# Layer b's scores in four row strips of the array, with one ring of five PSUM banks and a rearranged written order

## The chip, the cores and the metric

One core of a Trainium2 chip runs the whole program. The engines are TensorE (PE in the profile; its weight loads are PEld), VectorE (DVE), ScalarE (ACT), GpSimd (POOL) and SyncE (SP), which issues most of the DMA transfers. The metric is device microseconds of one execution. The kernel before took 4026.98 us, the median of three runs (4023.04 to 4030.02).

## The reference, cut to what matters

The input is four sequences of 2048 rows of 512 numbers. Four residual layers follow one another: layer a (linear attention), a feed-forward layer with int8 levels, layer b, and the same feed-forward layer again. The change touches layer b:

```python
g = sigmoid((x @ g_w.T + g_b).reshape(b, t, h, r))
decay = sigmoid(base_decay_logits)[None, :, :, None]
def step(M, inp):
    q_t, k_t, v_t, g_t = inp
    M = M * decay + einsum('bhr,bhd->bhrd', g_t * k_t * scale, v_t)
    y = einsum('bhr,bhrd->bhd', q_t, M)
    return (M, y)
```

There are 16 heads (h), each with a state of 16 x 32 (r x d), which decays at every row. q and k have 16 numbers per head and row. The outputs y of all rows go through a 512 x 512 product, are added to the row, and the sum is normalized.

## The kernel before, in words

All heavy arithmetic is in f32. Layer a with its feed-forward layer takes the first 2.4 ms of the span; layer b with its own runs from about 2450 us to the end. Layer b works on 32 blocks of 256 rows (NB = 4 sequences, 8 blocks each). A block has two halves of 128 rows (index i) and two groups of 8 heads (index g), so four **chunks**, numbered c = 2i + g. A sequence start clears the state (L1442).

A chunk does not step row by row. Within 128 rows, q and k are scaled by powers of the decay, and the chunk's work is:

- **scores** (L1318 to L1336): for each head, k times q over its 16 numbers gives a 128 x 128 matrix. A group's 8 heads lie on the 128 partitions, 16 apiece. Before the change, the scores are two matmuls (L1326), one for each half of the partitions: the stationary operand is k (64 rows by 128 columns, four heads in one), the moving one is q four times over (64 x 512), each copy zeroed by a mask for all heads but one (`q1`, L1294, with `head4`). Each fills one PSUM bank of `s`, which has two banks. Then L1333 starts the outputs `pyT` with the state's part, also in 64-row halves.
- **mask**: VectorE multiplies both banks by the causal triangle into `ab` (L1339), the last lines of `scores`.
- **update** (L1353, L1357): the state's growth, `pub`, added to `pairs`.
- **outputs** (L1366): scores times v, in 32-column strips, added to `pyT`; ScalarE copies it to `yT` (L1373), and GpSimd makes the next state (L1374).

The dense products of a block are features q and k for two groups (`pr`, L1230, 3.46 us of TensorE each), gates (`pg`) and the small maps `pl` (L1263), values (`pvb`, copied to `vb` by ScalarE, L1212), the output projection `py` (L1386) and the feed-forward product `pf` (L681). Each takes a PSUM bank from a ring with the tag `mm`, of three banks: a product's first matmul waits until the bank's holder three turns earlier has been read.

`prepare` (L1276 to L1303) makes the scaled operands of a group: k1 (L1282) and qs (L1288) on VectorE, q1 on ScalarE (L1294), ke and q0 on GpSimd (L1298). `turn_keys` then splits ke into 16-bit planes on VectorE (L710) and has SP's queue transpose them; `turned_keys` joins them on ScalarE (L717, kt). `turn_row` joins a transposed input row (xnTb, L717 too) and adds two biases on GpSimd (L1205, L1206).

The order on TensorE, VectorE, ScalarE and GpSimd is written by hand: within `tc.manual_schedule` an engine executes its instructions in the order in which `blocks_of(n)` issues them. In one call, `B` is the block whose chunks run, `after` the next (its features, gates, values and `prepare`), `later` the one after that (its rows are normalized and transposed), `before` the last (its output, normalization and feed-forward layer). Between two chunks' scores stand:

- chunk 0: features q 0, outputs of chunk 0, `levels(before, 0)`, features k 0, project(before, 1)
- chunk 1: weigh_output, gates and keys 0, outputs, `pf` of row 0, features q 1
- chunk 2: prepare 0, weigh_ffn, turn_row 0, values 0, turn_keys 0, outputs, `levels(before, 1)`, features k 1, project(B, 0)
- chunk 3: weigh_output, gates and keys 1, outputs, `pf` of row 1, store, prepare 1, turn_row 1, norm_output, turn_keys 1, values 1

Of the kernel before, what the change touches and what calls it, by code (L numbers as in the profile page):

```python
# [19 lines left out]
P = 128  # L20
# [12 lines left out]
HB, DB, R = 16, 32, 16  # L33
G = 2
HG = HB // G
# [6 lines left out]
QB = 128  # L42
NQ = P // QB
# [3 lines left out]
def hybrid_block_kernel(ctx: ExitStack, tc: tile.TileContext, t: dict, out: bass.AP):  # L47
# [4 lines left out]
    nc = tc.nc  # L52
    x_in = t["x"]
    NB, SEQ, _ = x_in.shape
# [581 lines left out]
    def run(steps):  # L636
        for f in steps:
            f()
# [432 lines left out]
    def layer_b_mild():  # L1071
        with ExitStack() as es:
# [4 lines left out]
            w = es.enter_context(tc.tile_pool(name="mb_w", bufs=1, reuse_waits="tile"))  # L1077
            pool = es.enter_context(tc.tile_pool(name="mb", bufs=2, reuse_waits="tile"))
            psum = es.enter_context(tc.tile_pool(name="mb_ps", bufs=1, space=PSUM, reuse_waits="tile"))

            bank = banks(psum, mm=3, s=2, y=2, u=1)
            at = [(b, blk) for b in range(NB) for blk in range(SEQ // TB)]

            def load_x(n):
# [20 lines left out]
                low[name] = soon.tile([P, 2, G, 2, 64], F32, name=f"low_{name}")  # L1105
                nc.sync.dma_start(low[name], t[f"m_{name}low"])
            small = {}
            for name in ("b_gb", "b_decay", "head4", "diag", "causal"):
                small[name] = w.tile(list(t[name].shape), F32, name=f"m_{name}")
                nc.sync.dma_start(small[name], t[name])  # L1110
            nc.sync.dma_start(wv, t["b_vT"].rearrange("(c p) n -> p c n", p=P))
# [164 lines left out]
            def prepare(B, g):  # L1276


                q, k = B.qk[g]
                A = Block()  # L1280
                A.k1 = pool.tile([P, NTB, NQ, P], F32, name=f"k1{g}", bufs=1)
                nc.vector.tensor_tensor(  # L1282
                    A.k1,
                    k.rearrange("p (i s) -> p i s", s=P).unsqueeze(2).to_broadcast([P, NTB, NQ, P]),
                    tk[:, g, :, :].unsqueeze(1).to_broadcast([P, NTB, NQ, P]), ALU.mult,
                )
                qs = pool.tile([P, NTB * NQ, QB], F32, name="qs", bufs=1)
                nc.vector.tensor_tensor(  # L1288
                    qs, q.rearrange("p (j s) -> p j s", s=QB),
                    tq[:, g, :].unsqueeze(1).to_broadcast([P, NTB * NQ, QB]), ALU.mult,  # L1290
                )
                A.q1 = pool.tile([P, NTB * NQ, 4, QB], F32, name=f"q1{g}", bufs=1)
                for h in range(4):
                    nc.scalar.activation(A.q1[:, :, h, :], qs, AF.Copy, scale=small["head4"][:, h : h + 1])  # L1294
                A.ke = pool.tile([P, NTB, P], F32, name="ke", bufs=1)
                A.q0 = pool.tile([P, NTB, P], F32, name=f"q0{g}", bufs=1)
                for dst, src, tab in ((A.ke, k, down), (A.q0, q, up)):
                    nc.gpsimd.tensor_tensor(  # L1298
                        dst, src.rearrange("p (i s) -> p i s", s=P),
                        tab[:, g, 1 : P + 1].unsqueeze(1).to_broadcast([P, NTB, P]), ALU.mult,  # L1300
                    )
# [11 lines left out]
            def chunk(B, i, g):  # L1313
# [4 lines left out]
                def scores():  # L1318


                    A = B.prep[g]
                    ps = [bank([P, NQ, 4, QB], F32, name="ps", tag="s") for _ in range(2)]
                    for j in range(NQ):
                        for half in range(2):
                            r = slice(half * 64, (half + 1) * 64)
                            nc.tensor.matmul(  # L1326
                                ps[half][:, j, :, :], A.k1[r, i, j, :], A.q1[r, NQ * i + j, :, :],
                                start=True, stop=True,
                            )
                    C.py = [bank([P, P], F32, name="pyT", tag="y") for _ in range(2)]  # L1330
                    for half in range(2):
                        r = slice(half * 64, (half + 1) * 64)
                        nc.tensor.matmul(  # L1333
                            C.py[half], st[r, half * P : (half + 1) * P], A.q0[r, i, :],
                            start=True, stop=False, skip_group_check=True,
                        )  # L1336
                    C.a = pool.tile([P, 2, 4, P], F32, name="ab")
                    for half in range(2):
                        nc.vector.tensor_tensor(  # L1339
                            C.a[:, half, :, :].rearrange("p h (j s) -> p h j s", s=QB),  # L1340
                            ps[half].rearrange("p j h s -> p h j s"),
                            small["causal"].rearrange("p (j s) -> p j s", s=QB).unsqueeze(1)
                            .to_broadcast([P, 4, NQ, QB]),
                            ALU.mult,
                        )

                def update():
# [13 lines left out]
                def outputs():  # L1361

                    for half in range(2):
                        for h in range(4):
                            lo = g * HG * DB + (4 * half + h) * DB
                            nc.tensor.matmul(  # L1366
                                C.py[half][h * DB : (h + 1) * DB, :], B.v[:, i, lo : lo + DB],
                                C.a[:, half, h, :], start=False, stop=True, skip_group_check=True,
                            )
                    if g == 0:  # L1370
                        B.yT[i] = pool.tile([P, KC, P], F32, name="yT", bufs=3)
                    for half in range(2):
                        nc.scalar.copy(B.yT[i][:, 2 * g + half, :], C.py[half])  # L1373
                    nc.gpsimd.tensor_tensor(  # L1374
                        st.rearrange("p (q c) -> p q c", c=2 * DB),
                        pairs[:, g, :].unsqueeze(1).to_broadcast([P, HG // 2, 2 * DB]),
                        small["diag"].rearrange("p (q c) -> p q c", c=2 * DB), ALU.mult,
                    )

                return scores, lambda: run([update, outputs])  # L1380

            def project(B, i):

# [1 line left out]
                for c in range(KC):  # L1385
                    nc.tensor.matmul(py, B.yT[i][:, c, :], wo[:, c, :], start=(c == 0), stop=(c == KC - 1))  # L1386

            def weigh_output(B, i):
                h = B.h[i] = pool.tile([P, D], F32, name="h")
                nc.vector.tensor_tensor(h, B.py.pop(i), B.xr[:, i, :], ALU.add)  # L1390
                B.stats[i] = stats(pool, h.unsqueeze(1), 1)

            def norm_output(B, i):
                h, x = B.h.pop(i), B.x[:, i, :]
# [43 lines left out]
            def blocks_of(n):  # L1438
# [3 lines left out]
                    nc.gpsimd.memset(state, 0.0)  # L1442
                    nc.gpsimd.memset(pairs, 0.0)
                nothing = lambda: None
                chunks = [chunk(B, c // G, c % G) if B else (nothing, nothing) for c in range(2 * G)]


                if B:
                    turned_keys(B, 0)
                chunks[0][0]()  # L1450
                if before:
                    weigh_ffn(before, 0)
                if after:
                    run(features(after, "q", 0))
                chunks[0][1]()
                if later:
                    weigh_row(later, 0)
                if before:
# [8 lines left out]
                    turned_keys(B, 1)  # L1467
                chunks[1][0]()
                if before:
                    weigh_output(before, 1)  # L1470
                if after:
                    run(gates(after, 0) + keys(after, 0))
                chunks[1][1]()
                if before:
                    run(before.levels[0])
                if later:
# [3 lines left out]
                if later:  # L1480
                    weigh_row(later, 1)
                if after:
                    run(features(after, "q", 1))


                chunks[2][0]()
                if after:
                    prepare(after, 0)
                if before:
                    weigh_ffn(before, 1)  # L1490
                if later:
                    turn_row(later, 0)
                if after:
                    run(values(after, 0))
                    turn_keys(after, 0)
                chunks[2][1]()
                if later:
                    norm_row(later, 1)
                if before:
# [7 lines left out]

                chunks[3][0]()
                if B:
                    weigh_output(B, 0)  # L1510
                if after:
                    run(gates(after, 1) + keys(after, 1))
                chunks[3][1]()
                if before:
                    run(before.levels[1])
                    store(before)
                if after:
                    prepare(after, 1)
                if later:
                    turn_row(later, 1)  # L1520
                if B:
                    norm_output(B, 0)
                if after:
# [17 lines left out]
def _constants(seq):  # L1541
# [10 lines left out]
        "head": (p[:, None] // R == np.arange(HG)[None, :]).astype(f),  # L1552
        "sub": (p[:, None] // SUB == np.arange(NS)[None, :]).astype(f),
        "diag": (p[:, None] // R == np.arange(HG * DB)[None, :] // DB).astype(f),
        "head4": (p[:, None] // R % 4 == np.arange(4)[None, :]).astype(f),
# [89 lines left out]
```

## Time and profile before

| what | value |
|---|---|
| median of three runs | 4026.98 us |
| the profiled execution | 4025.24 us |
| its span in the trace | 4023.4 us |
| granted TensorE clock, mean | 0.987 |
| one full block of layer b, scores to scores | 46.53 us |
| TensorE, VectorE, ScalarE, GpSimd busy in 2560 to 3950 us (1390 us) | 1356.2, 999.7, 325.9, 721.3 us |
| score matmuls L1326 | 512 records, 4 a chunk, 144.5 us busy |
| masks L1339 | 256, 684 ns each |
| q1 copies L1294 | 256, 497 ns each |

A line of the timeline gives start, length, engine, source line, operation, the tiles written and read, shapes and count; a bracket gives the engine's idle time just before, and what ended it. An f32 matmul leaves two records, one for each pass. A record's length contains the pipeline's tail, so that the distance of starts tells the time that a matmul takes from TensorE. Some tile names lose their numbers: `q<-qs,m_head` is q1, `k<-k,tk` is k1, `q<-q,up` is q0.

### The profile page before, as it was taken

The page shows a single profiled execution, that of the slowest core. Times are in us where ns is not written, and L with a number is a line of the kernel's source. Part 1 is how long each engine was busy: PE and PEld are TensorE (multiplying, and loading weights), DVE is VectorE, ACT ScalarE, POOL GpSimd, SP SyncE. Part 2 cuts the span into 40 slices and gives each one's busy share as a digit, 9 for nine tenths or more (in the row PEclk, how much of TensorE's full clock was granted, in tenths as well). Part 3 has the DMA queues.
Part 4 walks back from the last instruction along what each step waited for, and adds up shares of the span by engine and source line. Part 5 has one row for each costly group of instructions (what it writes and reads, how often), then busy time and mean ns, then how long its engine had stood idle before and what let it go on. Part 6 is the DMA issues. An engine that isn't in the chain of part 4 may idle for free.

```text
span 4023.4 us, 53593 instructions
## 1 busy us (share of the span) xinstructions
PE 3896.8 (97%) x20821; PEld 2133.2 (53%) x20821; DVE 2401.1 (60%) x4556; ACT 877.8 (22%) x1548; POOL 1516.3 (38%) x2527
## 2 busy tenths in 40 slices
PE   8999999999999999999999996999999999999996
PEld 4554554555554554555554544666556656665563
DVE  4455555555555555555555455677677767776775
ACT  2222222122122222222222211222222222222221
POOL 3233223323323322322332222455455545554553
PEclk9999999999999999999999997999999999999998
DMA  4122222212212212212212123122112111222111
GB/s 137 30 43 56 62 41 56 65 39 58 65 36 61 62 36 61 62 39 62 58 39 63 44 49 123 36 51 54 50 48 59 49 48 48 52 54 48 51 36 28
DMA packets 432040, 217.25 MB, mean 54 GB/s; under 512 B 363808, under 2 KB 376992, under 8 KB 431776
## 3 DMA queue, kind: packets, MB, share of 16 engines
q1 hardware_dynamic: 430656, 212.16, 21.7%
q8 instruction: 166, 2.72, 0.3%
q10 hardware_dynamic: 1120, 1.57, 0.1%
q14 instruction: 98, 0.80, 0.1%
HBM read 91.49 MB, written 34.08 MB: 31 GB/s over the span
## 4 chain that ended last, share of the span: by engine, by line
PE 90%; DVE 3%; ACT 2%; POOL 2%; DMA 2%; issue 1%; SPq 0%; ACTq 0%; POOLq 0%; DVEq 0%
PE pr L1230 12%; PE pk L648 11%; PE pv L648 11%; PE pq L648 11%; PE po L648 11%; PE py L1386 5%; PE pss L888 3%; PE pn L974 3%; PE pvb L648 3%; PE pg L648 3%; PE pl L1263 3%; PE pf L681 3%; PE pn L968 3%; PE ps L1326 3%; PE pu L904 2%
## 5 line engine op out<-in xcount | busy, mean ns | idle before, releaser
L648 PE MATMUL pq<-xnTa,a_Wq 128*128 128x512 f32 x1024 | 492.2, 608 | 0.0
L648 PE MATMUL pk<-xnTa,a_Wk 128*128 128x512 f32 x1024 | 491.0, 604 | 0.0
L126 POOL TENSOR_SCALAR rs<-mv 128x1 f32<-128x1 f32 x320 | 81.9, 256 | 1055.3 <-DVE mv L125 1052.2
L648 PE MATMUL pv<-a_Wv,xnTa 128*128 128x512 f32 x1024 | 476.3, 603 | 2.9 <-ACT xnTa L141 2.9
L648 PE MATMUL po<-a_Wo_sb,oT 128*128 128x512 f32 x1024 | 467.7, 601 | 6.4 <-DVE oT L950 6.4
L914 POOL TENSOR_TENSOR within<-state,u 64x64 f32<-64x64 f32 x256 | 155.8, 609 | 523.7 <-ACT u L909 514.1
L648 PEld LDWEIGHTS po<-a_Wo_sb,oT 128*128 128x128 f32 x1024 | 189.5, 190 | 235.3 <-issue 220.0
L648 PEld LDWEIGHTS pv<-a_Wv,xnTa 128*128 128x128 f32 x1024 | 188.7, 191 | 234.4 <-issue 224.2
L648 PEld LDWEIGHTS pq<-xnTa,a_Wq 128*128 128x128 f32 x1024 | 181.4, 189 | 193.1 <-issue 182.8
L648 PEld LDWEIGHTS pk<-xnTa,a_Wk 128*128 128x128 f32 x1024 | 184.5, 189 | 180.9 <-issue 158.8
L909 ACT COPY u<-pu 128x256 f32<-128x256 f32 x128 | 47.7, 373 | 1027.2 <-PE pu L904 1016.2
L1230 PE MATMUL pr<-xnTb,m_qT_sb 128*128 128x256 f32 x1024 | 240.6, 389 | 18.7 <-ACT xnTb L717 18.7
L1339 DVE TENSOR_TENSOR ab<-ps,m_causal 128x512 f32<-128x512 f32 x256 | 164.5, 684 | 131.6 <-PE ps L1326 131.6
L1230 PE MATMUL pr<-xnTb,m_kT_sb 128*128 128x256 f32 x1024 | 237.9, 385 | 0.0
L894 DVE TENSOR_TENSOR sm<-pss,causal 128x512 f32<-128x512 f32 x256 | 164.2, 683 | 119.4 <-PE pss L888 119.4
L648 PE MATMUL pvb<-b_vT_sb,xnTb 128*128 128x512 f32 x512 | 234.6, 601 | 0.0
L1386 PE MATMUL py<-b_oT_sb,yT 128*128 128x512 f32 x512 | 232.2, 596 | 0.0
L717 ACT COPY kr<-turned 128x1024 uint16<-128x1024 uint16 x120 | 139.3, 1161 | 425.6 <-DMA turned<-planes 425.6
L1230 PEld LDWEIGHTS pr<-xnTb,m_qT_sb 128*128 128x128 f32 x1024 | 196.1, 194 | 54.4 <-ACT xnTb L717 23.7
L683 DVE SCALAR_TENSOR_TENSOR f_y<-pf,f_sc,rscale 128x512 f32<-128x512 f32 x128 | 96.0, 750 | 198.3 <-PE pf L681 198.1
L1230 PEld LDWEIGHTS pr<-xnTb,m_kT_sb 128*128 128x128 f32 x1024 | 189.4, 190 | 35.6 <-issue 12.3
L127 POOL TENSOR_TENSOR rs<-rs,neg_half 128x1 f32<-128x1 f32 x320 | 193.1, 604 | 26.3
(158 smaller groups left out, 6304.0 us busy)
## 6 DMA issues: line engine op xcount, KB each, us to landing
wide<-rec SPq DMA_DIRECT2D x124, 256.0 KB, 3.7
mmid<-xa SPq DMA_DIRECT2D x16, 1024.0 KB, 4.3
out<-xb SPq DMA_DIRECT2D x32, 512.0 KB, 2.8
xa<-in_x SPq DMA_DIRECT2D x15, 1024.0 KB, 6.7
xb<-mmid SPq DMA_DIRECT2D x30, 512.0 KB, 3.8
turned<-planes SPq DMA_TRANSPOSE x304, 3.1
m_cos<-in_cos SPq DMA_DIRECT2D x30, 128.0 KB, 2.5
m_sin<-in_sin SPq DMA_DIRECT2D x30, 128.0 KB, 2.3
```

Source lines behind the costliest of these rows:

```text
L127: nc.gpsimd.tensor_tensor(rs, rs, neg_half[:, :n], ALU.pow)
L648: nc.tensor.matmul(held[0], lhs(), rhs(), start=(n == 0), stop=(n == len(pairs) - 1))
L681: nc.tensor.matmul(pf, qT[:, c, :], rq[:, c, :], start=(c == 0), stop=(c == KC - 1))
L717: nc.scalar.copy(dst.bitcast(U16).rearrange("p n (t two) -> p n t two", two=2), turned.rearrange("p (two n) t -> p n t two", two=2),)
L888: nc.tensor.matmul(ps[h][:, i, :], k[r, chunks[i]], q[r, chunks[i]], start=True, stop=True)
L894: nc.vector.tensor_tensor(s, ps[h], causal.unsqueeze(1).to_broadcast([P, NTA, P]), ALU.mult)
L914: nc.gpsimd.tensor_tensor(A.before[i + 1][r, r], A.before[i][r, r], u[r, i, :], ALU.add)
L968: nc.tensor.matmul(pn[:, i, :], A.before[i], q[:, chunks[i]], start=(i == 0), stop=False, skip_group_check=True,)
L974: nc.tensor.matmul(pn[r, i, :], v()[:, i, vh[h]], A.sm[h][:, i, :], start=False, stop=True, skip_group_check=True,)
L1230: nc.tensor.matmul(pr[:, half, :], wp[name][:, c, lo : lo + P], B.xnT[:, c, :], start=(c == 0), stop=(c == KC - 1),)
L1339: nc.vector.tensor_tensor(C.a[:, half, :, :].rearrange("p h (j s) -> p h j s", s=QB), ps[half].rearrange("p j h s -> p h j s"), small["cau ...
L1386: nc.tensor.matmul(py, B.yT[i][:, c, :], wo[:, c, :], start=(c == 0), stop=(c == KC - 1))
```

## The change

Each chunk's scores become four matmuls, one for each quarter (32 rows, two heads) of the partitions: k 32 x 128 stationary, q twice over moving (32 x 256, with `head2` in place of `head4`), each into a bank of its own. The banks for scores join those of the dense products in one ring of five, taken in the order in which the tiles are asked for. The mask becomes a step of its own, with four operations of 256 in place of two of 512; add_output, the sum of `py` and the row, is parted from weigh_output and goes ahead of the mask in chunks 1 and 3. values 0 and features q 1 change places. prepare 0 goes from chunk 2 to chunk 3 (behind the mask), turn_keys 0 from chunk 2 to the end of chunk 3, and turn_row 1 ahead of prepare 1.

```diff
-            bank = banks(psum, mm=3, s=2, y=2, u=1)
+            ring = banks(psum, mm=5, y=2, u=1)
+            def bank(shape, dtype, name, tag):
+                return ring(shape, dtype, name, "mm" if tag == "s" else tag)
...
-                for h in range(4):
-                    nc.scalar.activation(A.q1[:, :, h, :], qs, AF.Copy, scale=small["head4"][:, h : h + 1])
+                for h in range(2):
+                    nc.scalar.activation(A.q1[:, :, h, :], qs, AF.Copy, scale=small["head2"][:, h : h + 1])
...
-                    ps = [bank([P, NQ, 4, QB], F32, name="ps", tag="s") for _ in range(2)]
-                    for j in range(NQ):
-                        for half in range(2):
-                            r = slice(half * 64, (half + 1) * 64)
-                            nc.tensor.matmul(
-                                ps[half][:, j, :, :], A.k1[r, i, j, :], A.q1[r, NQ * i + j, :, :],
-                                start=True, stop=True,
-                            )
+                    C.ps = [bank([P, 2, P], F32, name="ps", tag="s") for _ in range(HG // 2)]
+                    for n in range(HG // 2):
+                        r = slice(n * 2 * R, (n + 1) * 2 * R)
+                        nc.tensor.matmul(C.ps[n], A.k1[r, i, :], A.q1[r, i, :, :], start=True, stop=True)
...
+                def mask():
+                    C.a = pool.tile([P, HG, P], F32, name="ab")
+                    for n in range(HG // 2):
+                        nc.vector.tensor_tensor(
+                            C.a[:, 2 * n : 2 * n + 2, :], C.ps[n],
+                            small["causal"].unsqueeze(1).to_broadcast([P, 2, P]), ALU.mult,
+                        )
...
                 chunks[1][0]()
                 if before:
+                    add_output(before, 1)
+                chunks[1][1]()
+                if before:
                     weigh_output(before, 1)
...
                 if after:
-                    run(features(after, "q", 1))
+                    run(values(after, 0))
                 chunks[2][0]()
-                if after:
-                    prepare(after, 0)
+                chunks[2][1]()
                 if before:
                     weigh_ffn(before, 1)
                 if later:
                     turn_row(later, 0)
                 if after:
-                    run(values(after, 0))
-                    turn_keys(after, 0)
-                chunks[2][1]()
+                    run(features(after, "q", 1))
+                chunks[2][2]()
...
                 chunks[3][0]()
                 if B:
+                    add_output(B, 0)
+                chunks[3][1]()
+                if B:
                     weigh_output(B, 0)
                 if after:
+                    prepare(after, 0)
                     run(gates(after, 1) + keys(after, 1))
-                chunks[3][1]()
+                chunks[3][2]()
                 if before:
                     run(before.levels[1])
                     store(before)
-                if after:
-                    prepare(after, 1)
                 if later:
                     turn_row(later, 1)
+                if after:
+                    turn_keys(after, 0)
+                    prepare(after, 1)
                 if B:
                     norm_output(B, 0)
```

More of the change, by code (lines that the diff above doesn't have):

```diff
@@ L1107, in layer_b_mild @@
             small = {}
-            for name in ("b_gb", "b_decay", "head4", "diag", "causal"):
+            for name in ("b_gb", "b_decay", "head2", "diag", "causal"):
                 small[name] = w.tile(list(t[name].shape), F32, name=f"m_{name}")
@@ L1280, in prepare @@
                 A = Block()
[L1281 to L1285, printed above, removed]
-                )
[L1287 to L1292, printed above, removed]
-                for h in range(4):
-                    nc.scalar.activation(A.q1[:, :, h, :], qs, AF.Copy, scale=small["head4"][:, h : h + 1])
+                A.k1 = pool.tile([P, NTB, P], F32, name=f"k1{g}", bufs=1)
+                qs = pool.tile([P, NTB, P], F32, name="qs", bufs=1)
+                for dst, src, tab in ((A.k1, k, tk[:, g, 0, :]), (qs, q, tq[:, g, :])):
+                    nc.vector.tensor_tensor(
+                        dst, src.rearrange("p (i s) -> p i s", s=P),
+                        tab.unsqueeze(1).to_broadcast([P, NTB, P]), ALU.mult,
+                    )
+                A.q1 = pool.tile([P, NTB, 2, P], F32, name=f"q1{g}", bufs=1)
+                for h in range(2):
+                    nc.scalar.activation(A.q1[:, :, h, :], qs, AF.Copy, scale=small["head2"][:, h : h + 1])
                 A.ke = pool.tile([P, NTB, P], F32, name="ke", bufs=1)
@@ L1321, in scores @@
                     A = B.prep[g]
-                    ps = [bank([P, NQ, 4, QB], F32, name="ps", tag="s") for _ in range(2)]
-                    for j in range(NQ):
-                        for half in range(2):
-                            r = slice(half * 64, (half + 1) * 64)
-                            nc.tensor.matmul(
-                                ps[half][:, j, :, :], A.k1[r, i, j, :], A.q1[r, NQ * i + j, :, :],
-                                start=True, stop=True,
-                            )
+                    C.ps = [bank([P, 2, P], F32, name="ps", tag="s") for _ in range(HG // 2)]
+                    for n in range(HG // 2):
+                        r = slice(n * 2 * R, (n + 1) * 2 * R)
+                        nc.tensor.matmul(C.ps[n], A.k1[r, i, :], A.q1[r, i, :, :], start=True, stop=True)
                     C.py = [bank([P, P], F32, name="pyT", tag="y") for _ in range(2)]
@@ L1336, in scores @@
                         )
-                    C.a = pool.tile([P, 2, 4, P], F32, name="ab")
-                    for half in range(2):
+                def mask():
+                    C.a = pool.tile([P, HG, P], F32, name="ab")
+                    for n in range(HG // 2):
                         nc.vector.tensor_tensor(
[L1340 to L1344, printed above, removed]
+                            C.a[:, 2 * n : 2 * n + 2, :], C.ps[n],
+                            small["causal"].unsqueeze(1).to_broadcast([P, 2, P]), ALU.mult,
                         )
@@ L1367, in outputs @@
                                 C.py[half][h * DB : (h + 1) * DB, :], B.v[:, i, lo : lo + DB],
-                                C.a[:, half, h, :], start=False, stop=True, skip_group_check=True,
+                                C.a[:, 4 * half + h, :], start=False, stop=True, skip_group_check=True,
                             )
@@ L1378, in outputs @@
                     )
-                return scores, lambda: run([update, outputs])
+                return scores, mask, lambda: run([update, outputs])
             def project(B, i):
@@ L1386, in project, with add_output, weigh_output @@
                     nc.tensor.matmul(py, B.yT[i][:, c, :], wo[:, c, :], start=(c == 0), stop=(c == KC - 1))
-            def weigh_output(B, i):
+            def add_output(B, i):
                 h = B.h[i] = pool.tile([P, D], F32, name="h")
                 nc.vector.tensor_tensor(h, B.py.pop(i), B.xr[:, i, :], ALU.add)
-                B.stats[i] = stats(pool, h.unsqueeze(1), 1)
+            def weigh_output(B, i):
+                B.stats[i] = stats(pool, B.h[i].unsqueeze(1), 1)
             def norm_output(B, i):
@@ L1444, in blocks_of @@
                 nothing = lambda: None
-                chunks = [chunk(B, c // G, c % G) if B else (nothing, nothing) for c in range(2 * G)]
+                chunks = [chunk(B, c // G, c % G) if B else (nothing, nothing, nothing) for c in range(2 * G)]
                 if B:
@@ L1450, in blocks_of @@
                 chunks[0][0]()
+                chunks[0][1]()
                 if before:
@@ L1454, in blocks_of @@
                     run(features(after, "q", 0))
-                chunks[0][1]()
+                chunks[0][2]()
                 if later:
@@ L1472, in blocks_of @@
                     run(gates(after, 0) + keys(after, 0))
-                chunks[1][1]()
+                chunks[1][2]()
                 if before:
@@ L1554, in _constants @@
         "diag": (p[:, None] // R == np.arange(HG * DB)[None, :] // DB).astype(f),
-        "head4": (p[:, None] // R % 4 == np.arange(4)[None, :]).astype(f),
+        "head2": (p[:, None] // R % 2 == np.arange(2)[None, :]).astype(f),
         "sin2": np.ascontiguousarray(
```

## The prediction

> **What bounds the kernel now.** I read the page's busy shares first, then the chain that ended last, then TensorE's waits from 2100 us on (where layer b lies), and last the timeline of single chunks.
>
> ```profile
> PE 3896.8 (97%) x20821; PEld 2133.2 (53%) x20821; DVE 2401.1 (60%) x4556; ACT 877.8 (22%) x1548; POOL 1516.3 (38%) x2527
> PE 90%; DVE 3%; ACT 2%; POOL 2%; DMA 2%; issue 1%; SPq 0%; ACTq 0%; POOLq 0%; DVEq 0%
> ```
>
> TensorE is busy 97% of the span and makes 90% of the chain. Inside layer b (the stretch 2560 to 3950 us) it is 1356.2 of 1390 us, with VectorE at 999.7 (72%) and GpSimd at 721.3 (52%). So a nanosecond off TensorE counts, unless another engine then comes late. What it waits for there:
>
> ```profile
> PE pr L1230 <- ACT xnTb L717: 18.7, 26, 0.7
> PE pyT L1333 <- POOL state_b L1442: 15.1, 3, 5.0
> PE pyT L1366 <- DVE ab L1339: 4.1, 6, 2.5
> ```
>
> Columns: us in all, times, longest. The first is one wait in nearly every block. The second is at the three later sequence starts. The third is the scores' mask, and the timeline puts it in the last block; in full blocks no mask is late.
>
> Layer b goes in blocks of four chunks. From the starts of L1326, chunk to chunk: 10.19, 12.68, 10.17, 13.49 us, 46.53 a block, the same to 0.01 us all along. The stretches of 12.68 and 13.49 hold the same amount of TensorE work (scores, three dense products of 3.45 us, outputs), so the first wait costs 0.81 us a block.
>
> **Part 1: the score matmuls.** The timeline of one chunk (start, length, engine, line):
>
> ```profile
> 3007.44 1.13 PE L1326 MATMUL ps<-q,k 64*128 64x512 f32 x4
> 3008.41 0.39 PE L1333 MATMUL pyT<-q,state_b 64*128 64x128 f32 x4
> 3008.72 1.99 PE L648 MATMUL pg<-xnTb,b_gT_sb 128*128 128x256 f32 x8
> 3010.65 0.65 PE L1263 MATMUL pl<-xc_q,low_q 128*64 128x256 f32 x4
> 3011.13 0.60 PE L1263 MATMUL pl<-xs_q,low_q 128*64 128x256 f32 x4
> ```
>
> Read starts, not lengths (lengths contain the pipeline's tail). An f32 matmul is two passes. The later L1263 groups, each two matmuls side by side on half arrays, follow every 0.43 us (3011.13, 3011.56, 3011.99): one 256-wide pass streams in 0.215 us, a 512-wide one in 0.43. py before them (eight 512-wide passes) takes 3.52 us from 3003.92 to 3007.44, 0.08 more than 8 x 0.43: about 0.09 us goes wherever the shape of the used array changes. The first group after such a change is also longer: 0.48 instead of 0.43, its second weights (64 columns) being loaded in the open; with 128 columns I take 0.11. The scores fit: 3007.44 to 3008.41 is 0.97 = 2 x 0.43 + 0.11, two 64-row matmuls abreast. L1333 follows in the same shape without the 0.09; it and its change to pg take 0.31.
>
> After: four matmuls of 32 rows, 256 wide, into four banks. If all four run abreast: 0.43 + 0.11, and 0.02 for staggered starts, is 0.56. Then a shape change that was not there, 32 to 64 rows: 0.09, and L1333's second load in the open, 0.05. So 0.56 + 0.14 + 0.31 = 1.01 instead of 1.28: **0.27 us saved a chunk**. The trace has pairs of row strips abreast (L1326, L1333) and quads of column strips (L1353, L1366), no quads of row strips. Bounds: with no price for the added change 0.41 saved; as two pairs one after the other 0.43 more streaming, so 0.16 lost; one by one 1.02 lost. I take 0.27, since pairs of both kinds and column quads run abreast.
>
> The skill has a rule against the part: the Trainium skill, "TensorEngine Tiling (Array Packing)", Key Properties, says that a change of tiling mode drains TensorE; "TensorE: Matmul & The Clock Gate", Single matmul latency, has a drain of about 175 ns. By that the added change would cost 0.175 in place of the rows' 0.09, an estimate of 0.19 saved a chunk instead of 0.27.
>
> **Part 2: masks and copies.** Two masks of 512 (0.684 us each) become four of 256; the nearest row is L1271, 256 wide and also from PSUM, at 0.42. Two started 0.61 apart, four should start 0.34 apart: 1.44 instead of 1.29 us on VectorE, +0.15 a chunk. Between mask and outputs TensorE has 3.5 us of dense work, so that hides; uncovered it would be 0.15 a chunk. ScalarE's copies of q per prepare go from four to two (0.43 each apart).
>
> The same tiling page's PSUM Bottleneck section warns that emptying PSUM can become the bound once matmuls are packed. By the page the masks would have to be late; in this trace VectorE waits for the scores (131.6 us over L1339), not TensorE for masks.
>
> **Part 3: the block's seam, where order and banks decide.** Around the start of a block:
>
> ```profile
> 3014.09 3.60 PE L648 MATMUL pvb<-b_vT_sb,xnTb 128*128 128x512 f32 x8
> 3014.29 0.75 DVE L683 SCALAR_TENSOR_TENSOR f_y<-pf,f_sc,rscale 128x512 f32<-128x512 f32 x1 [0.57 <-PE pf L681]
> 3014.96 0.41 DVE L1282 TENSOR_TENSOR k<-k,tk 128x256 f32<-128x256 f32 x1
> 3015.12 1.38 POOL L684 TENSOR_TENSOR xb<-xb,f_y 128x512 f32<-128x512 f32 x1 [0.60 <-DVE f_y L683]
> 3015.29 1.49 DVE L1288 TENSOR_TENSOR qs<-q,tq 128x256 f32<-128x256 f32 x1
> 3016.45 0.82 POOL L1298 TENSOR_TENSOR ke<-k,down 128x256 f32<-128x256 f32 x1
> 3016.87 1.71 ACT L1294 ACTIVATE q<-qs,m_head 128x256 f32<-128x256 f32 x4 [3.26 <-DVE qs L1288]
> 3017.61 1.13 PE L1326 MATMUL ps<-q,k 64*128 64x512 f32 x4
> 3018.48 1.15 ACT L717 COPY xnTb<-turned 128x1024 uint16<-128x1024 uint16 x1
> 3019.54 0.57 ACT L1212 COPY vb<-pvb 128x512 f32<-128x512 f32 x1
> ```
>
> L1288 takes 0.41 where GpSimd is quiet (start 3044.72) and 1.49 here: it ends 0.28 after GpSimd's add (3016.50). VectorE operations on two SBUF tiles, and copies, take turns with GpSimd's adds, each holding the other off. ScalarE waits for qs, copies four times, then turns xnTb; TensorE's next product starts at 3019.68, 5.59 after pvb's start.
>
> After, the turn of xnTb stands ahead of prepare: its wait goes. But the five-bank ring gives the product after the seam pvb's own bank (one turn later: pvb, four score tiles, then that product), so it now waits for vb's copy, and that stands on ScalarE behind the two q copies of prepare. From pvb's start: f_y ends at 0.95. VectorE now first turns ke (the moved step): it starts at 0.87 as L1282 did, 0.41 long, to 1.28. GpSimd's add ends 1.13 later, 2.41 (as 3015.37 to 3016.50). k1 to 2.70. GpSimd's next is now the ln_b add, alone 1.27, after a hold 1.14: 3.84. qs to 4.12, two copies 4.21 to 5.07, vb 0.57 to 5.64, TensorE at 5.69. It would be ready at 4.53 (3.52 for pvb and its change, 1.01 for scores and L1333). So the seam goes from 5.59 to **5.69, a loss of 0.10**: one wait takes the place of the other and eats chunk 0's saving as well.
>
> Queued behind that product on TensorE is everything; on ScalarE, behind vb, kt0, needed 3.5 us later.
>
> **The moved steps otherwise.** prepare(0), with two VectorE, two ScalarE and two GpSimd operations, goes from chunk 2 to chunk 3, 9 us ahead of its use. Its copies hold the gate's eviction about 1.5 us, before a use that waits for pl anyway; uncovered it would delay k by that. The turn of ke(0) goes behind the store in SP's queue: issued about 2.7 after pvb's start, landing 3.1 later (median of these transposes), copied by ScalarE near 6.3, used at 9.2. add_output, now ahead of the mask, frees py's bank: pg needs it 0.2 + 0.68 + 0.05 = 0.93 after py's streaming end and arrives 1.10 after. values(0) and features q1 change places, equal in length (3.45).
>
> In the chunk-2 stretch VectorE has xc_q and xs_q (1.36) ahead of its levels, and the third score tile of chunk 3 waits for xs_k at the end of that row. Now it ends at 3053.74, 0.24 ahead of the scores. Added 1.36 less 0.33 (pairs had begun 0.38 after pub, the first of these can at 0.05); taken away up to 1.9, as planes (1.67 against 0.70 alone) and f_xn (1.49 against 0.53) may come after GpSimd's adds. So between 0.8 late and 1.1 early. I take no wait, since planes and f_xn come later by those 1.03 us while GpSimd's adds (from 3047.22 on) do not.
>
> **The sum.** 31 full blocks: chunks 1 to 3 save 3 x 0.27, 25.1 us. The seam is a wait of this sort in 27 of them: +2.7 (the sequence starts stay tied to GpSimd's queue and the 5.0 us wait, their chunk 0 gains nothing). Net -22.4. The profiled execution took 4025.24 us with a span of 4023.4, the median is 1.7 above it: 4025.24 - 22.4 = 4002.8. I say 4003.
>
> **Rivals.**
> - *The seam's hold does not happen* (0.14): k1 and qs pass before GpSimd's second add. Then vb ends by 4.3, TensorE goes at 4.53: 1.06 off 5.59, x 27 = 28.6 more than part 1's 25.1: 3971.5. For it: L1288 does run in 0.41 at some places. Against: GpSimd's ops stand back to back here.
> - *The seam is held one turn more* (0.12), the slower case: qs misses the gap after the ln_b add and waits out out_b's too, 1.42 x 27 = 38.3: 4041. The point from which it decides: vb ending later than 6.5, as 27 x 0.93 is what chunks 1 to 3 save.
> - *Four strips run as two pairs* (0.09): the change does not do what it says; 93 x 0.16 lost, and 2.7: 4043. One by one: 4123, 0.02 of the 0.09.
> - *VectorE late at chunk 3* (0.06): 0.7 x 31 = 21.7 given back, 4024.5: no change.
> - Forecast as worked out: 0.59, between 3985 (no price for the change of strips, 0.41 x 93 = 38) and 4017.
>
> **Chances.** Within 0.2% (8 us, about what a measurement of this kernel can tell from no change): the last rival and 0.03 of the forecast. Slower: 0.21. Faster: 0.14 + 0.56 = 0.70. The range 3967 to 4041 takes in all but the serial case and half of the two rivals at 4041 to 4043, with something below.
>
> **What would show it.** L1325 with eight records, first start to L1329's near 0.65 us; the three short stretches of a block shorter by 0.27 each; a wait of TensorE at the seam named vb (L1216) in place of xnTb, about 1.1 us; L1288 at about 1.4 there. Wrong, if the score records come in two groups, or TensorE waits for xs_k (L1242) or masks (L1337) in full blocks.

## The result and the profile after

The changed kernel takes **4009.36 us** (median, 4008.33 to 4011.99); the kernel before took 4023.78 in the same comparison (4021.37 to 4030.02). The ratio is 0.9962, with a 95% interval of 0.995 to 0.9975: faster, by 14.4 us (0.4%). The forecast was 4003.0, in a range of 3967 to 4041. Of the two profiled executions, before took 4025.24 us and after 4008.33; the spans are 4023.4 and 4006.5, so the traces have 16.9 us to explain, at the same mean clock (0.987 and 0.988).

The page of the changed kernel, busy shares and shares of the chain:

```profile
PE 3870.2 (97%) x21333; PEld 2125.5 (53%) x21333; DVE 2430.6 (61%) x4812; ACT 832.9 (21%) x1420; POOL 1498.1 (37%) x2527
PE 90%; DVE 4%; DMA 2%; POOL 2%; issue 1%; ACT 1%; SPq 0%; ACTq 0%; POOLq 0%; DVEq 0%
```

TensorE has 512 records more and 26.6 us of busy time less; it is still the bound. Of its waits from 2100 us on (us in all, times, longest), these bear on layer b's blocks:

```profile
PE pr L1234 <- ACT vb L1216: 25.0, 26, 1.0
PE pyT L1329 <- POOL state_b L1439: 16.8, 3, 5.6
PE pyT L1361 <- DVE ab L1337: 4.6, 2, 2.9
PE pg L648 <- DVE xs_k L1242: 0.4, 1, 0.4
```

The first line is the wait of nearly every block. It has a new releaser: the copy of the values (L1216) where the turned row stood before. The second is at the three later sequence starts as before, 5.61 us each instead of 5.02. The mask is waited for only in the last block, and xs_k once, in the first block (at 2515.5 us): neither in a full block.

The timeline of a chunk's scores (L1325 and L1329 are L1326 and L1333 of before):

```profile
2999.97 0.71 PE L1325 MATMUL ps<-q,k 32*128 32x256 f32 x8
3000.61 0.49 PE L1329 MATMUL pyT<-q,state_b 64*128 64x128 f32 x4
3001.03 1.99 PE L648 MATMUL pg<-xnTb,b_gT_sb 128*128 128x256 f32 x8
```

Four strips leave eight records. The first passes of the four start at 2999.969, .976, .982 and .989, so all four run abreast; scores to L1329 is 0.64, scores to pg 1.06 (1.28 before). Four masks take 1.42 and nothing waits for them.

And the seam of a block; first the line of the kernel before in which its wait ends, then the changed kernel:

```profile
3019.68 3.72 PE L1230 MATMUL pr<-xnTb,m_qT_sb 128*128 128x256 f32 x16 [0.72 <-ACT xnTb L717]
```

```profile
3006.40 3.60 PE L648 MATMUL pvb<-b_vT_sb,xnTb 128*128 128x512 f32 x8
...
3007.43 1.38 POOL L684 TENSOR_TENSOR xb<-xb,f_y 128x512 f32<-128x512 f32 x1 [0.61 <-DVE f_y L683]
3007.60 1.49 DVE L1288 TENSOR_TENSOR k<-k,tk 128x256 f32<-128x256 f32 x1
3008.77 1.45 POOL L1209 TENSOR_TENSOR xb<-xb,b_ln_b_row 128x512 f32<-128x512 f32 x1
3009.01 1.48 DVE L1288 TENSOR_TENSOR qs<-q,tq 128x256 f32<-128x256 f32 x1
3010.59 0.91 ACT L1294 ACTIVATE q<-qs,m_head 128x256 f32<-128x256 f32 x2 [3.61 <-DVE qs L1288]
3011.41 0.56 ACT L1216 COPY vb<-pvb 128x512 f32<-128x512 f32 x1
3012.02 3.72 PE L1234 MATMUL pr<-xnTb,m_qT_sb 128*128 128x256 f32 x16 [0.96 <-ACT vb L1216]
```

GpSimd's two adds (L684, L1209) hold k1 and qs in turn, the q copies wait for qs, vb stands behind them, and the next product needs vb's bank. From pvb's start to that product is 5.62 us (5.59 before).

From chunk to chunk, the stretches of a full block, with the kernels of the experiments (each of them differs from the changed kernel as its section says; ratios are against the kernel before):

| kernel | median us | ratio, 95% interval | chunk 1→2 | 2→3 | 3→0 | 0→1 (seam) | block |
|---|---|---|---|---|---|---|---|
| before | 4023.78 | | 10.19 | 12.68 | 10.17 | 13.49 | 46.53 |
| changed | 4009.36 | 0.9962 (0.995 to 0.9975) | 9.96 | 12.49 | 9.96 | 13.52 | 45.92 |
| e1, values first | 3990.40 | 0.9909 (0.9893 to 0.9926) | 10.25 | 12.49 | 9.96 | 12.49 | 45.18 |
| e2, adds later | 3993.02 | 0.9917 (0.99 to 0.9933) | 9.96 | 12.49 | 9.96 | 12.89 | 45.29 |
| e3, scores twice | 4047.74 | 1.0054 (1.0038 to 1.0071) | 10.39 | 12.92 | 10.38 | 13.52 | 47.21 |
| e7, turn back | 4019.76 | 0.9984 (0.9974 to 0.9993) | 9.96 | 12.49 | 9.96 | 13.95 | 46.35 |
| e9, halves | 4005.55 | 0.9951 (0.9937 to 0.9965) | 10.17 | 12.70 | 10.17 | 12.70 | 45.74 |
| e8, e1 and e2 | 3982.95 | 0.9892 (0.9877 to 0.9907) | 9.96 | 12.49 | 9.96 | 12.49 | 44.89 |
| e4, add behind | 4019.41 (one run) | | 10.10 | 12.49 | 10.10 | 13.52 | 46.21 |
| e5, prepare back | 4029.36 | 1.0009 (1.0 to 1.0019) | 9.96 | 12.49 | 10.72 | 13.52 | 46.67 |

In the runs of the experiments the kernel before took 4025.3 to 4025.7 us, against 4023.8 beside the changed kernel. A difference of medians between an experiment and the changed kernel is therefore sure to about 2 us only; the stretches, from the traces, are surer.

Stretches 1→2, 2→3 and 3→0 lost 0.235, 0.194 and 0.214 us and the seam gained 0.03, which makes 0.616 a block. Over 26 full blocks that is 16.0 of the 16.9 us. The rest: the first two blocks -1.26, the three blocks of later sequence starts +0.36, the way to layer b's first scores -1.06, the last block +1.23, the end -0.15.

### The profile page after: what moved, and what is told of

Its sections match the earlier page's. It is cut to its first block, busy times and chain, and to the rows that moved or that the text cites. A ratio compares the mean times of both kernels' runs of the same rounds, so it can differ in the third digit from the quotient of the medians.

```text
span 4006.5 us, 54782 instructions
## 1 busy us (share of the span) xinstructions
PE 3870.2 (97%) x21333; PEld 2125.5 (53%) x21333; DVE 2430.6 (61%) x4812; ACT 832.9 (21%) x1420; POOL 1498.1 (37%) x2527
## 4 chain that ended last, share of the span: by engine, by line
PE 90%; DVE 4%; DMA 2%; POOL 2%; issue 1%; ACT 1%; SPq 0%; ACTq 0%; POOLq 0%; DVEq 0%
PE pr L1234 12%; PE pq L648 11%; PE pk L648 11%; PE pv L648 11%; PE po L648 11%; PE py L1381 5%; PE pss L888 3%; PE pn L974 3%; PE pg L648 3%; PE pl L1267 3%; PE pf L681 3%; PE pvb L648 3%; PE pn L968 3%; PE pu L904 2%; PE ps L1325 2%; PE pyT L1361 1%
## 5 line engine op out<-in xcount | busy, mean ns | idle before, releaser
L838 DVE TENSOR_TENSOR xa<-po,xa 128x512 f32<-128x512 f32 x64 | 44.1, 689 | 258.6 <-PE po L648 258.6
```

## The experiments

My theory: the strips save about 0.21 us in each chunk; at the seam vb's copy, behind the q copies that GpSimd's adds hold off, has taken the place of the turned row and eats chunk 0's share. Rivals: the strips do not run abreast, and the gain is the order's alone; the seam is late for another reason (the turned row still, or the ring itself); the moves of prepare 0 and add_output do nothing.

### e1: values ahead of prepare 1

Only ScalarE's order of vb's copy and the q copies changes by this (on TensorE, values 1 stays behind the same work).

```diff
                 if after:
                     turn_keys(after, 0)
+                    run(values(after, 1))
                     prepare(after, 1)
                 if B:
                     norm_output(B, 0)
                 if after:
                     turn_keys(after, 1)
-                    run(values(after, 1))
```

> Only ScalarE's order changes against the changed kernel: at the seam vb's copy (L1216) stands ahead of prepare 1's two q copies. Theory (the product after the seam waits for vb, and vb stands behind copies that wait for qs): vb can then be read 4.2 us after pvb's start, TensorE is ready at about 4.6, the wait for vb (1.0 us each, 25.0 in all) goes, and the seam falls from 5.62 to about 4.6. Part of it should come back one step later: in the changed kernel xs_k ends 0.84 us ahead of chunk 1's scores, and it hangs on GpSimd's last add, which does not move, so that the third score strip then waits about 0.2 us. Net about 0.8 us a block, 27 blocks: 3986 to 3993 us. Rival (the product waits for something else that ends at the same time, a transfer or xnTb): no change, 4009.

Measured, as my theory expected: 3990.40 us, 19.0 under the changed kernel. The wait for vb is gone, and the seam's stretch equals the other long one (12.49). One thing is late in its place. The timeline of the next chunk 1:

```profile
3018.21 0.68 DVE L1242 TENSOR_TENSOR xs_k<-pr,m_sin 128x512 f32<-128x512 f32 x1
3018.69 1.00 PE L1325 MATMUL ps<-q,k 32*128 32x256 f32 x8
...
3019.63 0.49 PE L1329 MATMUL pyT<-q,state_b 64*128 64x128 f32 x4
```

xs_k ends at 3018.89, 0.20 after the first strip's start. Three strips start at 3018.694, .700 and .707, the fourth at 3019.034, after xs_k's end (it needs the bank that xs_k reads; e8 shows the wait gone where xs_k is early); L1329 follows 0.94 after the scores instead of 0.64. In the changed kernel xs_k was 0.84 ahead here; the seam's 1.03 us less overtook it. So the wait for vb did cost 1.03 us a block, and 0.295 of it comes back as this wait.

### e2: the bias adds of the turned row later

The two adds on GpSimd (L1209, L1210) are parted from turn_row and issued behind norm_output; vb stays where it was.

```diff
                 if later:
-                    turn_row(later, 1)
+                    turn_row(later, 1, late=True)
                 if after:
                     turn_keys(after, 0)
                     prepare(after, 1)
                 if B:
                     norm_output(B, 0)
+                if later:
+                    bias_row(later, 1)
```

> Against the changed kernel GpSimd's two bias adds of turn_row 1 (L1205, L1206 before) go behind norm_output's two operations; ScalarE's and VectorE's orders stay. Theory (VectorE's two-tile operations and GpSimd's adds take turns): qs then waits out ke (0.5) and not an add (1.14), L1288 takes about 0.85 there and not 1.48, and the seam falls from 5.62 to about 5.0: 0.6 us in 27 blocks, 3993 us, if nothing behind it is late; rs of weigh_ffn now stands behind the two adds on GpSimd, which can give back some tenths a block. Rival (qs is slow there for another reason, or its length does not matter): L1288 stays at 1.48, the seam at 5.62, 4009 us.

Measured, as expected: 3993.02. The seam's timeline (lines stand 4 further down here; L1292 is qs, L1220 vb):

```profile
3005.78 0.85 DVE L1292 TENSOR_TENSOR qs<-q,tq 128x256 f32<-128x256 f32 x1
...
3007.54 0.56 ACT L1220 COPY vb<-pvb 128x512 f32<-128x512 f32 x1
3008.16 3.72 PE L1238 MATMUL pr<-xnTb,m_qT_sb 128*128 128x256 f32 x16 [0.33 <-ACT vb L1220]
```

qs takes 0.85 instead of 1.48, and the wait for vb falls from 0.96 to 0.33. The ln_b add in front of qs was two thirds of the wait; the ring and the orders of TensorE, VectorE and ScalarE were untouched, so these alone do not make the whole wait.

### e3: the score matmuls twice

Each strip is computed a second time into the same bank, with the same values.

```diff
-                    for n in range(HG // 2):
+                    for n in list(range(HG // 2)) * 2:
```

> Each chunk's four score matmuls are issued a second time into the same banks (same values). Theory (four strips stream abreast, 2 x 0.215 us for all four, weights of the second set loaded under the first): 0.43 us more in each of chunks 1 to 3; at the seam the wait for vb hides it (ready at 5.0 against 5.62). 93 x 0.43 = 40: 4049 us. Rival (two pairs one after the other): 0.86 more a chunk, 4089 us and the seam late too; one by one 1.7 a chunk, over 4160 us.

Measured, as expected of four abreast: 4047.74, 38.4 more than the changed kernel; a block takes 1.296 more, three times 0.432.

The doubled group in the timeline, sixteen records:

```profile
3013.24 1.15 PE L1325 MATMUL ps<-q,k 32*128 32x256 f32 x16
3014.31 0.49 PE L1329 MATMUL pyT<-q,state_b 64*128 64x128 f32 x4
```

A second set of four costs two passes of 0.216, the time of one strip: four are abreast, at no price among themselves. In pairs it would have been twice as much. The seam's stretch stays at 13.52: there the wait for vb shrinks from 0.96 to 0.53, so whatever the scores take or save at the seam is swallowed by it.

### e7: the turned row back behind prepare 1

```diff
-                if later:
-                    turn_row(later, 1)
                 if after:
                     turn_keys(after, 0)
                     prepare(after, 1)
+                if later:
+                    turn_row(later, 1)
```

> Against the changed kernel turn_row 1 goes back behind prepare 1, its place before the change. Theory (what stands ahead of vb on ScalarE sets the seam): ScalarE does two q copies, then xnTb (1.16), then vb; qs waits out ke and not an add, so q copies end near 4.45, xnTb 5.5, vb 6.05, TensorE at 6.1 after pvb's start against 5.62: 0.5 us in 27 blocks, 4022 us. Rival (the early turn_row does not matter): 4009 us.

Measured, close to what was expected: 4019.76, 10.4 more than the changed kernel. TensorE's waits:

```profile
PE pr L1234 <- ACT vb L1216: 36.5, 27, 1.4
```

With the old place of the turned row, vb stands behind it too, and the seam takes 13.95, although qs, with the bias adds behind it, now takes 0.85 instead of 1.48. So the move of turn_row is worth 0.43 us a block, net of what it costs qs.

### e9: two halves again, ring and order kept

Part 1 is undone: two 64-row matmuls of 512 into two banks, four q copies, two masks of 512; the ring of five and the new order stay.

```diff
-                    C.ps = [bank([P, 2, P], F32, name="ps", tag="s") for _ in range(HG // 2)]
-                    for n in range(HG // 2):
-                        r = slice(n * 2 * R, (n + 1) * 2 * R)
+                    C.ps = [bank([P, 4, P], F32, name="ps", tag="s") for _ in range(2)]
+                    for n in range(2):
+                        r = slice(n * 64, (n + 1) * 64)
```

> Part 1 of the change undone, the rest kept: scores in two 64-row halves of 512 with four q copies, in the ring of five and in the new order. Theory (the score strips save 0.22 a chunk, but their four banks put pvb's bank in the way of the product after the seam): each of the chunks 1 to 3 costs 0.19 to 0.24 more, as before the change (10.19, 12.68, 10.17); but with two banks a chunk the product after the seam takes pl's bank, not pvb's, and xnTb is early, so that the seam has no wait: 12.68 in place of 13.52. A block 45.72 us: 4025 - 27 x 0.81 = 4003 us, faster than the changed kernel though its scores are slower. Rival (the seam is late through VectorE or GpSimd, whatever the banks): seam near 13.5, 4025 us.

Measured, near the expected time: 4005.55, which is a time that the intervals do not part from the changed kernel's; by blocks it is 0.18 us quicker. The seam:

```profile
3007.16 3.60 PE L648 MATMUL pvb<-b_vT_sb,xnTb 128*128 128x512 f32 x8
3010.69 1.13 PE L1325 MATMUL ps<-q,k 64*128 64x512 f32 x4
3011.97 3.72 PE L1234 MATMUL pr<-xnTb,m_qT_sb 128*128 128x256 f32 x16
3013.11 0.56 ACT L1216 COPY vb<-pvb 128x512 f32<-128x512 f32 x1
```

The product goes 1.28 after the scores, with no wait, though vb is copied 1.14 **later** than that: with two score tiles in the ring, this product does not get pvb's bank. So order and ring alone take 0.79 us off a block (46.53 to 45.74), about the 0.81 of the old wait. No run parts the ring from the order, or tries the exchange of values 0 with features q 1 or the later turn_keys 0 by itself. The four strips, in this order, save 3 x 0.21 and put vb in the way at the seam for 0.82: they earn nothing.

### e8: e1 and e2 together

> Both edits of the two earlier runs on the changed kernel: vb's copy ahead of prepare 1's q copies, and turn_row 1's two bias adds behind norm_output on GpSimd. Theory: with vb first the seam is free of waits (12.49 us from chunk 0's scores to chunk 1's); what that run lost again, 0.29 us a block, was chunk 1's fourth score strip waiting for xs_k, which hangs on GpSimd's last add; with the bias adds out of its way that add comes 1.5 us earlier and the wait goes. A block is then 2 x 9.96 + 2 x 12.49 = 44.89 us against 45.18: 26 x 0.29 = 7.6 us less than with vb first alone, 3982 us. Rival (the 0.29 is something else, a price of the seam itself): 3990, and the fourth strip still comes late.

Measured, as expected: 3982.95, 26.4 under the changed kernel and 1.1% under the kernel before. No wait for vb is left, and xs_k of chunk 1 is early again: it ends 1.4 us ahead of the scores. A block takes 44.887; against e9, with no wait at either seam, that is 0.855 less, or 0.214 a chunk. This is the strips' worth by itself, four times over.

### e4: add_output behind the mask

```diff
                 chunks[3][0]()
+                chunks[3][1]()
                 if B:
                     add_output(B, 0)
-                chunks[3][1]()
```

(and the same in chunk 1).

> Against the changed kernel add_output goes back behind the mask in chunks 1 and 3. Theory (in the ring of five pg takes py's bank right after the scores): pg waits until four masks (1.42 us) and the add (0.69) are done, near 2.8 us after the scores' start against 1.06 now: 1.75 us twice a block, 31 blocks: 4117 us. Rival (another engine gives pg cover): under 4030 us.

A miss: 4019.41 in its one run, a block 0.29 longer. The timeline of a chunk:

```profile
3006.72 0.71 PE L1325 MATMUL ps<-q,k 32*128 32x256 f32 x8
3007.45 1.42 DVE L1337 TENSOR_TENSOR ab<-ps,m_causal 128x256 f32<-128x256 f32 x4 [0.95 <-PE ps L1325]
3007.93 1.99 PE L648 MATMUL pg<-xnTb,b_gT_sb 128*128 128x256 f32 x8
3008.79 0.68 DVE L1385 TENSOR_TENSOR h<-py,xr 128x512 f32<-128x512 f32 x1
```

pg starts 1.21 after the scores, before the add (L1385) has even begun. It starts right after the first mask (3007.45 + 0.42): it took the first **score** bank, not py's. So the ring does not go by fixed turns, as I had read it (for the ring of three of the kernel before, too). What fits is that a new tile gets the bank whose release comes first in the written order: in the changed kernel that order and the turns agree, and here the mask is written ahead of the add. This rule is read from one run. The rival's time (under 4030) came true; cover from another engine, its reason, does not show in this trace. The add's move was thus worth 0.15 us in each of two chunks, not a long wait.

### e5: prepare 0 back to chunk 2

```diff
                 chunks[2][1]()
+                if after:
+                    prepare(after, 0)
...
                 if after:
-                    prepare(after, 0)
                     run(gates(after, 1) + keys(after, 1))
```

> Against the changed kernel prepare 0 goes back to chunk 2, right behind its mask. Theory (VectorE has 1.2 us idle there before xc_q, and xs_k ends 0.24 us ahead of chunk 3's scores): its two VectorE operations fit into the idle time, but its two GpSimd operations push the bias adds of turn_row 0 back by about 1.1 us, and they hold xr, planes and f_xn; xs_k ends about 0.2 us later and the last strips of chunk 3 wait 0 to 0.3 us: 4009 to 4018 us. Rival (that stretch of VectorE has no room): over 0.8 us a block late, 4034 us and more.

A miss in size: 4029.36, 20.0 more than the changed kernel, and all of it in one stretch: chunk 3 to 0 takes 10.72 instead of 9.96. The timeline ahead of chunk 3:

```profile
3003.36 1.64 DVE L710 COPY planes<-xr 128x1024 uint16<-128x1024 uint16 x1
3004.42 1.17 POOL L1369 TENSOR_TENSOR state_b<-pairs,m_diag 128x256 f32<-128x256 f32 x1
3004.93 0.94 DVE L131 TENSOR_SCALAR f_xn<-xb,mv,rs 128x512 f32<-128x512 f32 x1
...
3008.48 0.68 DVE L1242 TENSOR_TENSOR xs_k<-pr,m_sin 128x512 f32<-128x512 f32 x1
3008.50 1.47 PE L1325 MATMUL ps<-q,k 32*128 32x256 f32 x8
```

prepare's operations on GpSimd push its adds back. planes takes 1.64 instead of 1.10 and f_xn 0.94 instead of 0.53 (held by the state's product, L1369, and not by the bias adds that I had named), and xs_k ends 0.66 after the scores' start instead of 0.24 ahead. Three strips go on time, the fourth 0.81 after the first, and L1329 follows at 1.40 instead of 0.64. In the changed kernel's order, having prepare 0 elsewhere buys those 20 us; this is what the prediction's rival "VectorE late at chunk 3" describes. In the kernel before, prepare 0 stood in chunk 2 with xs_k 0.24 ahead, so e5 does not price that place in the old order.

## Why the prediction was right, step by step

**Part 1, the strips.** Abreast, as predicted: scores to L1329 0.64 (0.65 forecast), e3 shows the four at the price of one. The **mis-sized term** is "L1329's second load in the open, 0.05". L1329's passes start 0.213 apart, where the forecast had 0.16. Three spacings agree on the size. The scores' passes are 0.320 apart, 0.215 of streaming and 0.105 more; L1329's 128-wide passes 0.213, 0.107 of streaming and 0.106 more; in e3 the second set of scores, with no change of shape before it, follows at 0.216, with nothing more. So after a change of shape one load of weights lies in the open, for about 0.106 where it has 128 columns. That it is the second, as the forecast has it, is not what the load records suggest. The first loads start with the first passes (2999.967 and 2999.969), the second loads 0.109 later (3000.076), and the second passes 0.213 after these (3000.289), just as in e3 without a change (load 3013.557, pass 3013.772). The open load is thus more likely the first, counted inside the first pass; for the sum it makes no difference. My 0.05 came from a group with 64 columns, though L1329's weights have 128 (I had allowed 0.11 for the scores' own). With 0.11 the sum gives 0.21 saved; e8 against e9 measures 0.214. The change of shape itself was right: scores' second pass to L1329 is 0.324, 0.215 of streaming and 0.109 more, where I had 0.09. By the Trainium skill's drain ("TensorEngine Tiling (Array Packing)", Key Properties, with "TensorE: Matmul & The Clock Gate", Single matmul latency) this would be 0.175, an estimate; the measured 0.109 is less. The load in the open costs as much again.

**Part 2.** Masks at 1.42 (1.44 forecast), hidden everywhere in full blocks.

**Part 3, the seam.** 5.62 where 5.69 was forecast and 5.59 was before; the wait for vb is 0.96 (1.1 forecast), k1 1.49, qs 1.48 (1.4). The chain of the forecast is the chain of the trace, instruction by instruction, and e1 and e2 break it at two links. The rival in which qs passes ahead of the add gave 3971.5; e2 and e8 take the ln_b add out of qs's way by order (3993 and 3983).

**The moved steps.** No wait for xs_k at chunk 3: xs_k ends 0.24 ahead of the scores, as before; e5 shows that the margin is real. planes and f_xn fell from 1.67 and 1.49 to 1.10 and 0.53, as the forecast thought they might, but xr, which it had not named, rose from 0.54 to 1.14; that all this comes out at the old 0.24 is partly luck. The strip that waits when xs_k is late is the fourth (e1, e5), not the third. add_output's place was of use, but for 0.15 us a chunk (e4), and the reason given, py's bank, holds only while the add is written ahead of the mask.

**The sum.** Forecast -22.4, measured -16.9 in the traces. The strips gave 0.643 a block instead of 0.81 (26 blocks: 4.3 less), the seam lost 0.03 instead of 0.10 (1.9 back). At the three later sequence starts I had 0.81 gained each, and they lost 0.36 together: 2.8 less. There the wait for GpSimd takes part, and this stretch differs from one start to the next (20.0, 20.8 and 21.2 us in the changed kernel, 20.8, 20.4 and 20.2 in e1). Why it varies stays open. The last block's +1.23 and the way to the first scores, -1.06, had no term and cancel by luck. One figure of the forecast does not come out of its own terms: the 3985 at the low end of the worked-out case should be 3990 (4025.24 less 0.41 x 93, and 2.7 back).

**What the sign rested on.** The forecast put the gain on the strips (25.1 us) and a loss on the seam (2.7). That is right for the change as a whole against before, but e9 shows it can be split otherwise: order and ring alone bring the same 0.4 to 0.5%, and the strips add something only in a better order (e1, e2, e8). That the new order and ring would bring the whole net gain without the strips was not forecast.

## What to carry to other kernels

A shared ring of PSUM banks turns the number of tiles a step asks for into a wait somewhere else: list, for each new holder of a bank, who must have read it and what that reader stands behind on its own engine. When a wait goes, ask at once what was second; here one wait of 0.8 us was replaced by another of the same size, and moving the reader one step ahead (e1) was worth more than the change. Narrower strips pay by their streaming, here 0.430 us a chunk, less 0.109 for the change of shape and 0.105 for the load in the open.

## What the runs showed of the hardware

- Four f32 matmuls of 32 rows run fully abreast, their starts 7 ns apart; another set of four costs 0.432 us (e3). If one of the four is late by its bank, the other three go ahead, but the step ends late by nearly the whole delay: 0.34 late, 0.295 lost (e1).
- VectorE operations on SBUF tiles and GpSimd's adds hold each other in turns: qs, 256 wide, takes 0.41 alone, 0.85 beside GpSimd's 0.82 of ke (e2) and 1.48 behind an add of 512; the ln_b add takes 1.27 where it goes first (e5, 3001.77) and 1.45 behind k1 (the seam above). f_xn, a one-input operation on SBUF, is held as well (0.53 at 2995.91 in the changed kernel, 0.94 in e5), while the masks, which read PSUM, were not (0.41 to 0.43 in all 512 of the changed kernel). The Trainium skill, "SBUF — State Buffer", Who interferes with whom, has VectorE and GpSimd contend for a shared port pair where VectorE reads two SBUF inputs or runs in a two-port mode, and the second to issue blocks until the first is done. The rows of qs and the ln_b add agree with that; in which mode f_xn runs, no trace here shows.
